# A two-layer graph network on one core: product 4 of the score projection split a second time by Strassen's scheme

## The chip, the cores and the metric

One core of a Trainium2 chip. The number that counts is the device time of one execution in microseconds (us); a single core runs, so it is that core's time. The engines are TensorE (PE in the profile, with its weight loads as PEld), VectorE (DVE), ScalarE (ACT), GpSimd (POOL) and SyncE (SP, which here only issues DMAs). Everything is fp32, apart from one product that uses fp32r.

## The reference

```python
# x: (64, 256, 512), adj: (256, 256) of zeros and ones, weights 512 x 512
h = max(layernorm(x), 0)
q, k, v = h @ Wq.T, h @ Wk.T, h @ Wv.T
rel = adj.T[None] * (q @ k.T)                 # per batch entry, 256 x 256
rel = rel / norm(rel, axis=2, keepdims=True)
x = x + rel @ v
h = max(layernorm(x), 0)
x = x + (einsum('nm,bmd->bnd', adj, h) @ weight + bias)
```

## The kernel before

The kernel takes the 64 batch entries two at a time: 32 pairs of 512 tokens. `M = Wq.T @ Wk` is made once, so the scores of a pair are `h M h.T`. For a pair there are: the transposed `h` (tile `ht`), G = the transpose of `h M` (tile `g`), V (tile `v`), the scores (`rel`), the attention product that is added to x, the second layer norm, y = adj times h2 (tile `yt`, "gather", in fp32r with h2 split into an upper and a lower part), and the product of y with the last weight, added to x ("mix").

Each large product is done by Strassen's scheme in Winograd's form: the two operands are cut in 2 x 2 blocks, sums of blocks are formed (the `left_factors` and `right_operands`, four sums each), and seven products of blocks take the place of eight. A product by one level here is 128x128 weights against 256 columns, four matmuls. The products of one result share a PSUM bank where one's value goes into the next: `bank_a` collects products 1, 6, 7 and 4, and after each of them VectorE or ScalarE takes the running sum out (`take`). For G, V and the mix, products 2 and 3 are split once more (`two_levels`, steps `g1` to `g4`): seven products of 128x128 against 128 columns, for 2 and 3 at once (`both`), in `bank_e` and `bank_d`, added into the first quarter of the result by VectorE (`add`). `bank_e` uses only its first half.

The second-level sums of the weights are made once by POOL (`second_right`). Those of h are made for each pair by VectorE (`second` in `new_ht`, called `h_second`, rows L176 to L179 with the tile `hs`). One level below, `sums` are the four first-level sums of h (rows L176 to L179 with the tile `ht`); the third gives factor 6, the fourth factor 3.

The transposes of h go by DMA and VectorE: `place_blocks` moves 32x32 blocks of h into the tile `blocks` (SP's queue), and `transpose_blocks` turns them, eight instructions a pair (L453). The last quarter of `blocks` is also scratch space of `norm_by_scalar` on ScalarE. `ident` is a 128x128 identity for transposes by matmul at the start and at the end.

The order of work on PE, DVE and ACT is the order of the code (`manual_schedule`); only waits on data are added. `run_steps` runs a list of PE steps, and after step n whatever stands in slot n of a dictionary. In `steady`, which makes 28 of the 32 pairs' rounds, one round is: `attend_and_v` (attention of pair i mixed with the rest of V of pair i+1), `scores` of pair i+1, `g_and_v` of pair i+2, the gather of pair i, and `mix_and_v`. What a slot holds is a matter of when VectorE and ScalarE get to it. In `g_and_v` the PE order is G's products 1, 5, 6 with g1, V's 1, G's 7 with g2, V's 5, G's 4 with g3; g4 of G comes in the mix. The bias is added to x by POOL (`add_bias`, L736), four adds a pair that wait only for their data: each may start when ScalarE's relu of the same chunk has read x (`relu_of`, L345). L566 is the mask (adjacency times scores), L580 the reciprocal of the norm, L583 the scaling of the scores, L720 and L724 the upper and lower part of h2. L469 and L490 are VectorE's takes and adds for G, L177 with the tile `yt` is the sum of y that product 5 of the mix needs.

Of the kernel before, what the change touches and what calls it, by code (L numbers as in the profile page):

```python
# [9 lines left out]
F32 = mybir.dt.float32  # L10
# [9 lines left out]
def kernel(  # L20
# [38 lines left out]
    nc = tc.nc  # L59
    P = 128  # L60
    B, N, D = x.shape
    DC = D // P
    NC = N // P
    NB = 2
# [5 lines left out]
    HC = DC // 2  # L70
# [8 lines left out]
    small = ctx.enter_context(tc.tile_pool(name="small", bufs=3))  # L79
    ps_m = ctx.enter_context(tc.tile_pool(name="ps_m", bufs=8, space=bass.MemoryType.PSUM))  # L80

    X, H, HL, G, V, R, H2, Y, HL2, Y2, second_h, own_steps = ({} for _ in range(12))

    ring = [const.tile([P, NB, NC, D], F32, name=f"x_ring{n}") for n in range(5)]
    blocks = const.tile([P, TC, DC, P], F32, name="blocks")
# [60 lines left out]
        t = const.tile([P, 3, HC, HD], F32, name=f"{name}_t")  # L146
        return right_operands(right_blocks(w), [t[:, n] for n in range(3)])

    def second_right(right, name):


        factors, steps = {}, []
        for n in (2, 3):
            t = const.tile([P, 3, P], F32, name=f"{name}_t{n}")
            factors[n], more = right_operands(
                lambda j, k, f=right[n]: f[:, j, ts(k, P)], [t[:, r] for r in range(3)], nc.gpsimd
            )
            steps += more
        return factors, steps

    def run(steps):
        for step in steps:
            step()
# [45 lines left out]

        return [(lambda args=args: step(*args)) for args in order]  # L210

    def two_levels(product, take, matmul, add):

        bank_a = ps_m.tile([P, 512], F32, tag="pm", name="bank_a")
        bank_c = ps_m.tile([P, 512], F32, tag="pm", name="bank_c")
        bank_d = ps_m.tile([P, 512], F32, tag="pm", name="bank_d")  # L220
        bank_e = ps_m.tile([P, 512], F32, tag="pm", name="bank_e")
        by_k = bank_d.rearrange("p (k s n) -> p k s n", k=2, s=2)
        at_b, at_c = by_k[:, :, 0], by_k[:, :, 1]
        at_a = bank_e[:, : 2 * P].rearrange("p (k n) -> p k n", k=2)

        def both(at, n, start=False):
            for k in range(2):
                matmul(at[:, k], k + 2, n, start and k == 0)

        def a1():  # L230
            product(bank_a, 1, True)
            take(0, 0, bank_a, True)

        def c5():
            product(bank_c, 5, True)
            take(1, 1, bank_c, True)

        def a6():
            product(bank_a, 6, False)
            take(0, 1, bank_a, True)  # L240

        def c():
            take(0, 1, bank_c, False)

        def a7():
            product(bank_a, 7, False)
            take(1, 1, bank_a, False)

        def a4():
            product(bank_a, 4, False)  # L250
            take(1, 0, bank_a, True)

        def g1():
            both(at_a, 1, True)
            both(at_c, 5, True)
            add(0, 0, at_a)
            add(1, 1, at_c)

        def g2():
            both(at_a, 6)  # L260
            both(at_c, 3)
            add(0, 1, at_a)

        def g3():
            both(at_a, 7)
            both(at_b, 2)
            add(1, 1, at_a)
            add(0, None, bank_d)

        def g4():  # L270
            both(at_a, 4)
            add(1, 0, at_a)

        return dict(a1=a1, c5=c5, a6=a6, c=c, a7=a7, a4=a4, g1=g1, g2=g2, g3=g3, g4=g4)

    def winograd(product, take, side={}, early=False):

# [126 lines left out]
    def new_ht(i):  # L404


        hh = twice.tile([P, DC * NC + 3 * HC, HT_], F32, tag="ht", name=f"ht_{i}")
        ht = hh[:, : DC * NC].rearrange("p (d h) n -> p d h n", h=NC)
        pair = hh[:, DC * NC : DC * NC + 2 * HC].rearrange("p (d e) n -> p d e n", e=2)
        HL[i], sums = left_factors(left_blocks(ht), [hh[:, DC * NC + 2 * HC :], pair[:, :, 1], pair[:, :, 0]])  # L410

        def second():
            room = work.tile([P, 4, 2, P], F32, tag="hs2", name=f"hs2_{i}")
            two = hh[:, HC * NC : DC * NC + 2 * HC].rearrange("p (w d e) n -> p w d e n", w=2, e=2)
            factors, steps = left_factors(
                lambda b, d: two[:, :, d, 0, ts(b, P)], [room[:, n] for n in range(4)]
            )
            HL2[i] = {k: {n: f[:, k - 2] for n, f in factors.items()} for k in (2, 3)}
            return steps

        second_h[i] = second
        return ht, sums

    def transposes_by_matmul(i):
# [51 lines left out]
    def g_by_two_levels(i):  # L476
        product, take = g_product(i)
        g = G[i].rearrange("p (k e) t n -> p k e t n", k=2)

        def matmul(out, k, n, start):  # L480
            nc.tensor.matmul(  # L481
                out, m_second[k][n], HL2[i][k][n], start=start, stop=True, skip_group_check=True
            )

        def add(b, e, sums):
            if e is None:
                dst, sums = G_all[:, :, 0, ts(b, P)], sums.rearrange("p (c n) -> p c n", c=DC)
            else:
                dst = g[:, :, e, 0, ts(b, P)]
            nc.vector.tensor_add(dst, sums, dst)  # L490

        G_all = G[i]
        return two_levels(product, take, matmul, add)

    def spare_blocks():

# [48 lines left out]
    def scores(i, side={}, by_matmul=False, inside=False, own=False):  # L545
# [61 lines left out]
        def turn_at_once():  # L607
            for b in range(NB):
                pt = ps_m.tile([P, T], F32, tag="pm", name="pr")
                for t in range(NC):  # L610
                    for k in range(NC):
                        nc.tensor.transpose(
                            pt[:, ts(t * NC + k, P)], rel[:, b, k, ts(t, P)], ident
                        )
                nc.scalar.copy(turned[:, b].rearrange("p t k n -> p (t k n)"), pt)

# [114 lines left out]
    def add_bias(i):  # L731

        xt = flat(X[i])
        add = nc.gpsimd.tensor_tensor
        return [
            (lambda c=c: add(xt[:, c, :], xt[:, c, :], bias_bc, ALU.add)) for c in range(TC)  # L736
        ]
# [169 lines left out]
    m_right, m_steps = weight_operands(m_sb, "m")  # L907
    wv_right, wv_steps = weight_operands(wvt_sb, "wv")
    w_right, w_steps = weight_operands(w_sb, "w")
    m_second, m_second_steps = second_right(m_right, "m2")  # L910
    wv_second, wv_second_steps = second_right(wv_right, "wv2")
    w_second, w_second_steps = second_right(w_right, "w2")
    in_order = {EngineType.PE, EngineType.DVE, EngineType.Activation}
# [14 lines left out]
    def g_and_v(i, side):  # L928

        g, v = g_by_two_levels(i), v_by_two_levels(i)  # L930
        run_steps([
            g["a1"], g["c5"], lambda: run([g["a6"], g["g1"]]), v["a1"],
            lambda: run([g["c"], g["a7"], g["g2"]]), v["c5"], lambda: run([g["a4"], g["g3"]]),
        ], side)
        return g, v

    def mix_and_v(i, g, v, side):


        m = mix_by_two_levels(i)  # L940
        run_steps([
            m["a1"], m["c5"], lambda: run([m["a6"], m["c"]]), lambda: run([m["g1"], v["a6"]]),
            lambda: run([m["a7"], m["g2"], g["g4"], v["c"]]), lambda: run([m["a4"], m["g3"]]),
        ], side)
        return m

    def first_pairs(exact):
# [42 lines left out]
            0: sums2[1:2], 1: sums2[2:3], 2: sums2[3:4],  # L990
        })
        stats, *parts = ln1(0, exact)
        h_second = second_h.pop(2)()
        attend(0, by_slot({c: [stats[c]] for c in range(TC)}, {
            0: masks[0:1], 1: masks[1:2] + squares[0:2], 2: squares[2:4] + [norm_root],
        }))
# [1 line left out]
        if exact:  # L998
            nc.vector.tensor_copy(adjt_r, adjt_sb)
        g, v = g_and_v(2, by_slot(layer_1(parts), {  # L1000
            1: h_second + [inverse], 2: turned3[0:4], 3: scales + [place],
            4: add_bias(0) + turned3[4:6], 5: turned3[6:8], 6: sums3[0:1],
        }))
        v_steps, rel_steps = attend_operands(1)
        y_products, y_steps = gather_steps(0, exact)
# [13 lines left out]
    def steady(i, exact, relu0, v_last, mixed, v):  # L1019
# [13 lines left out]
        if i + 4 < NP:  # L1033
            load(i + 4)
        HL2.pop(i + 1)
        h_second = second_h.pop(i + 2)()
        masks, squares, norm_root, inverse, scales, place, turns = scores(i + 1, {
            0: halves[2:3], 1: halves[3:4] + h_second[0:1], 2: [root] + h_second[1:4],
            3: [end] + relus[0:1], 4: relus[1:2],
        }, inside=True, own=True)  # L1040
        turned, sums = transpose_blocks(i + 3)
        v_steps, rel_steps = attend_operands(i + 1)
        g, v = g_and_v(i + 2, {
            0: masks + squares + [norm_root] + turned[0:4] + [inverse] + scales + [place],
            1: uppers[0:2] + lowers[0:2],
            2: relus[2:4],
            3: uppers[2:4] + turned[4:8],
            4: lowers[2:3] + sums[0:1] + add_bias(i),
            5: own_steps[i + 1][0:2] + lowers[3:4] + sums[1:3],
            6: own_steps[i + 1][2:4] + sums[3:4] + v_steps[0:1],  # L1050
        })
        y_products, y_steps = gather_steps(i, exact)
        run_steps(y_products, {0: v_steps[1:2], 2: y_steps[0:1], 3: turns})
# [14 lines left out]
    def last_pairs(exact, relu0, v_last, mixed, v):  # L1068
# [6 lines left out]
            0: v_last, 1: gs[0:1], 2: gs[1:2], 3: gs[2:3], 4: gs[3:4] + halves[0:1],  # L1075
            5: halves[1:2],
        })
        h_second = second_h.pop(c)()
        masks, squares, norm_root, inverse, scales, place, turns = scores(b, {
            0: halves[2:3], 1: halves[3:4] + h_second[0:1], 2: [root] + h_second[1:4],  # L1080
            3: [end] + relus[0:1], 4: relus[1:2],
        }, inside=True)
        g, v = g_and_v(c, {
            0: masks + squares + [norm_root, inverse] + scales + [place],
            1: uppers[0:2] + lowers[0:2],
            2: relus[2:4],
            3: uppers[2:4],
            4: lowers[2:3] + add_bias(a),
            5: lowers[3:4],
        })  # L1090
        y_steps = gather(a, exact)
        g["g4"]()
        gs = g_operands(c, spare_blocks())
        run_steps([v["a6"], v["g1"], v["a7"], v["g2"], v["a4"], v["g3"]], {
            0: gs[0:2] + [v["c"]], 1: gs[2:3], 2: gs[3:4], 3: y_steps[0:1], 4: y_steps[1:3],
# [83 lines left out]
```

## Time and profile before

| | |
|---|---|
| time, median of 3 runs | 1700.23 us (1699.68 to 1700.37) |
| profiled execution, its own time | 1700.89 us |
| its span, first to last instruction | 1699.1 us |
| TensorE clock granted, mean | 0.999 |
| one steady round (scores at 768.35 to scores at 820.08) | 51.73 us |
| in it busy: PE / DVE / ACT / POOL | 51.73 / 45.88 / 27.47 / 6.71 us |
| in its G stage (820.08 to 834.77): PE / DVE / ACT / POOL | 14.69 / 10.95 / 11.44 / 5.49 us |

The busy time of an engine is the union of its instructions' spans. Instructions of VectorE overlap a little, as do those of TensorE: a 128x512 sum lasts 0.68 us, and the next starts 0.60 us after it. So where cost is asked, the distance from start to start counts and not the duration. A wait in brackets at the end of a timeline line is the engine's idle time just before, with the instruction whose end is held to have released it. In the view of waits a line gives the total in us, how often, and the longest.

### The profile page before, as it was taken

The page shows a single profiled execution, that of the slowest core. Times are in us where ns is not written, and L with a number is a line of the kernel's source. Part 1 is how long each engine was busy: PE and PEld are TensorE (multiplying, and loading weights), DVE is VectorE, ACT ScalarE, POOL GpSimd, SP SyncE. Part 2 cuts the span into 40 slices and gives each one's busy share as a digit, 9 for nine tenths or more (in the row PEclk, how much of TensorE's full clock was granted, in tenths as well). Part 3 has the DMA queues.
Part 4 walks back from the last instruction along what each step waited for, and adds up shares of the span by engine and source line. Part 5 has one row for each costly group of instructions (what it writes and reads, how often), then busy time and mean ns, then how long its engine had stood idle before and what let it go on. Part 6 is the DMA issues. An engine that isn't in the chain of part 4 may idle for free.

```text
span 1699.1 us, 28457 instructions
## 1 busy us (share of the span) xinstructions
PE 1685.2 (99%) x10274; PEld 1530.6 (90%) x10274; DVE 1474.9 (87%) x3312; ACT 856.7 (50%) x1947; POOL 227.1 (13%) x191
## 2 busy tenths in 40 slices
PE   9999999999999999999999999999999999999998
PEld 7988999999999999999999999999999999999986
DVE  7788898888898888898888988888988889888777
ACT  4455445655545555446555456554465544564331
POOL 1211100111101111001111011110011110011111
PEclk9999999999999999999999999999999999999999
DMA  7413332233322233322333322333223333223101
GB/s 245 63 28 85 83 77 51 47 82 85 78 60 64 52 84 85 75 55 57 67 85 81 77 48 49 85 84 76 57 64 58 84 82 78 51 44 60 38 25 53
DMA packets 395270, 118.89 MB, mean 70 GB/s; under 512 B 367600, under 2 KB 368368, under 8 KB 395120
## 3 DMA queue, kind: packets, MB, share of 16 engines
q1 hardware_dynamic: 382528, 76.60, 24.1%
q0 software_dynamic: 8432, 32.51, 5.2%
q10 hardware_dynamic: 4160, 7.87, 1.3%
q8 instruction: 83, 1.36, 0.3%
q14 instruction: 67, 0.55, 0.1%
HBM read 38.27 MB, written 33.55 MB: 42 GB/s over the span
## 4 chain that ended last, share of the span: by engine, by line
PE 96%; DVE 3%; DMA 0%; issue 0%; ACT 0%; ACTq 0%; DVEq 0%
PE bank_a L302 25%; PE bank_a L290 13%; PE bank_a L314 7%; PE py L752 7%; PE bank_c L302 7%; PE bank_e L528 6%; PE bank_a L675 6%; PE bank_d L528 5%; PE bank_c L290 3%; PE bank_c L314 3%; PE bank_e L481 3%; PE bank_c L675 3%; PE bank_d L481 2%; PE bank_b L314 2%; PE bank_b L675 1%; PE pu L636 1%
## 5 line engine op out<-in xcount | busy, mean ns | idle before, releaser
L736 POOL TENSOR_TENSOR x_ring<-x_ring,bias_bc 128x512 f32<-128x512 f32 x128 | 187.6, 1486 | 667.6 <-DVE rel L563 436.3
L302 PE MATMUL bank_a<-wv_t,ht 128*128 128x256 f32 x768 | 181.7, 379 | 0.0
L290 PE MATMUL bank_a<-ht,m_t 128*128 128x256 f32 x768 | 181.4, 379 | 0.0
L290 PEld LDWEIGHTS bank_a<-ht,m_t 128*128 128x128 f32 x768 | 145.9, 190 | 19.8
L302 PEld LDWEIGHTS bank_a<-wv_t,ht 128*128 128x128 f32 x768 | 143.5, 190 | 18.3
L516 ACT COPY v<-bank_a 128x512 f32<-128x512 f32 x96 | 55.1, 574 | 206.5 <-PE bank_a L302 206.5
L724 DVE TENSOR_TENSOR h<-h2c,h 128x512 fp32r<-128x512 f32 x128 | 85.5, 691 | 80.1 <-ACT h L720 80.1
L367 ACT ACTIVATE blocks<-x_ring,sm 128x512 f32<-128x512 f32 x112 | 80.9, 722 | 119.4 <-DVE sm L364 117.6
L345 ACT ACTIVATE h2c<-x_ring,nb,rs 128x512 f32<-128x512 f32 x128 | 97.3, 808 | 59.7 <-DVE nb L342 50.0
L752 PE MATMUL py<-adjt_r,h 128*128 128x256 f32 x1024 | 126.0, 280 | 0.5 <-DVE h L724 0.4
L302 PE MATMUL bank_a<-w_t,ys 128*128 128x256 f32 x512 | 121.4, 380 | 0.4 <-DVE x_ring L786 0.3
L752 PEld LDWEIGHTS py<-adjt_r,h 128*128 128x128 f32 x1024 | 119.8, 188 | 1.0 <-DVE h L724 0.9
L807 POOL DMA_DIRECT2D out_dram<-x_ring x31 | 24.1, 776 | 720.5 <-issue 521.2
L380 ACT ACTIVATE h<-x_ring,nb,rs 128x512 f32<-128x512 f32 x112 | 82.0, 802 | 66.0 <-PE bank_e L528 66.0
L302 PEld LDWEIGHTS bank_a<-w_t,ys 128*128 128x128 f32 x512 | 96.8, 190 | 14.3 <-DVE x_ring L786 1.0
L786 DVE TENSOR_TENSOR x_ring<-bank_a,x_ring 128x512 f32<-128x512 f32 x128 | 88.0, 687 | 22.6 <-PE bank_a L302 22.5
L314 PE MATMUL bank_a<-ht,gt 128*128 128x128 f32 x744 | 101.2, 279 | 0.0
L561 ACT COPY rel<-bank_a 128x256 f32<-128x256 f32 x96 | 35.8, 373 | 129.7 <-PE bank_a L314 107.3
L333 DVE BATCH_NORM_STATS2 st<-x_ring 128x6 f32<-128x512 f32 x144 | 97.8, 679 | 0.4
L756 ACT COPY yt<-py 128x512 f32<-128x512 f32 x128 | 75.1, 588 | 45.4 <-PE py L752 44.5
L314 PEld LDWEIGHTS bank_a<-ht,gt 128*128 128x128 f32 x744 | 90.4, 192 | 3.0
L453 DVE STREAM_TRANSPOSE ht<-blocks 128x256 f32<-128x256 f32 x248 | 87.8, 409 | 0.8 <-DMA blocks<-h 0.8
(224 smaller groups left out, 4064.7 us busy)
## 6 DMA issues: line engine op xcount, KB each, us to landing
blocks<-h SPq DMA_DIRECT2D x496, 64.0 KB, 2.3
out_dram<-x_ring POOLq DMA_DIRECT2D x31, 1024.0 KB, 4.8
x_ring<-in_x_dram SPq DMA_DIRECT2D x28, 1024.0 KB, 5.7
placed<-rel SPq DMA_DIRECT2D x384, 32.0 KB, 2.0
x_ring<-in_x_dram ACTq DMA_DIRECT2D x4, 1024.0 KB, 5.4
wq_sb<-in_L_gnn_Wq_dram SPq DMA_DIRECT2D x4, 256.0 KB, 4.9
wk_sb<-in_L_gnn_Wk_dram ACTq DMA_DIRECT2D x4, 256.0 KB, 6.3
wv_sb<-in_L_gnn_Wv_dram ACTq DMA_DIRECT2D x1, 1024.0 KB, 5.8
```

The lines of the kernel that those rows point to most:

```text
L290: nc.tensor.matmul(bank[:, e * HT_ : (e + 1) * HT_], right[n][:, d, ts(e, P)], left[n][:, d, :], start=(start and e == 0 and d == 0), stop ...
L302: nc.tensor.matmul(bank[:, b * HD : (b + 1) * HD], left[n][:, d, ts(b, P)], right[n][:, d, :], start=(start and b == 0 and d == 0), stop=( ...
L314: nc.tensor.matmul(bank[:, ts(b, P)], right[n][:, d, ts(b, P)], left[n][:, d, ts(b, P)], start=(start and b == 0 and d == 0), stop=(d == H ...
L333: nc.vector.bn_stats(st[:, c, :], src[:, c, :])
L345: nc.scalar.activation(dst, src[:, c, :], AF.Relu, bias=nb[:, c : c + 1], scale=rs[:, c : c + 1])
L453: nc.vector.transpose(ht[:, d, half].rearrange("p (b n) -> p b n", b=NB), by_half[:, :, half, d])
L528: nc.tensor.matmul(out, left[k][n], right[k][n], start=start, stop=True, skip_group_check=True)
L675: nc.tensor.matmul(bank[:, ts(b, HD)], left[n][:, b], right[n][:, b], start=(start and b == 0), stop=True, skip_group_check=True,)
L724: nc.vector.tensor_sub(dst[:, 1, c, :], whole_h[c], dst[:, 0, c, :].bitcast(F32))
L736: (lambda c=c: add(xt[:, c, :], xt[:, c, :], bias_bc, ALU.add)) for c in range(TC)
L752: nc.tensor.matmul(pm[:, d, :], left[:, b * NC + m, ts(d0 + d, P)], right, start=(n == 0), stop=(n == len(terms) - 1),)
L786: nc.vector.tensor_add(xt[block], bank.rearrange("p (b e) -> p b e", b=NB), xt[block])
```

## The change

Product 4 of G is split a second time, like 2 and 3. Its seven quarter products are distributed so: numbers 2, 3 and 4 go straight into `bank_a` at the places of their quarters; numbers 1 and 5 go into the free second half of `bank_e`, and so do later 6 and 7, on top of 1. Steps `h1` (five matmuls, in the place of `a4`), `h1_sums` (two VectorE adds at the end of slot 6), `h2` (after product 5 of the mix) and `h3` (just ahead of `g4`).

For this, four sums of h at the second level are made for each pair (`fourth`, called `h_four`; they lie in the first quarter of `blocks`, once the transposes have read it), and four sums of the weight once more on POOL, one of which overwrites `ident`; so the last transposes by matmul take an identity made anew in `v_room`.

Other work moves. `h_second` goes from the scores to slot 0 of G, and the last two first-level sums of h from slots 5 and 6 of G to the scores of the next round (`late`). The transposes go from slots 0 and 3 to 1 and 3. Precision and data of the other products are as before.

```diff
-    def second_right(right, name):
+    def second_right(right, name, room=None):
         factors, steps = {}, []
-        for n in (2, 3):
-            t = const.tile([P, 3, P], F32, name=f"{name}_t{n}")
+        for n in (2, 3) if room is None else (2, 3, 4):
+            rooms = 3 if n < 4 else 2
+            t = const.tile([P, rooms, P], F32, name=f"{name}_t{n}")
+            t = [t[:, r] for r in range(rooms)] + [room]
...
+        four_a, four_c = bank_e[:, 2 * P : 3 * P], bank_e[:, 3 * P :]
+
+        def h1():
+            for n, at in ((2, 0), (3, 2), (4, 1)):
+                matmul(bank_a[:, ts(at, P)], 4, n, False)
+            matmul(four_a, 4, 1, False)
+            matmul(four_c, 4, 5, False)
+            take(1, 0, bank_a, True)
+
+        def h1_sums():
+            add_to_four(0, 0, four_a)
+            add_to_four(None, 1, four_c)
+
+        def h2():
+            matmul(four_a, 4, 6, False)
+            add_to_four(0, 1, four_a)
+
+        def h3():
+            matmul(four_a, 4, 7, False)
+            add_to_four(1, None, four_a)
...
+        def fourth():
+            room = blocks.rearrange("p c d e -> p (c d) e")
+            HL2[i][4], steps = left_factors(
+                lambda b, d: HL[i][4][:, d, ts(b, P)], [room[:, n] for n in range(4)]
+            )
+            return steps
...
+        def add_to_four(b, e, sums):
+            if b is None:
+                dst = G_all[:, e, 1, :].rearrange("p (b n) -> p b n", b=NB)
+            elif e is None:
+                dst = G_all[:, :HC, 1, ts(b, P)]
+            else:
+                dst = G_all[:, e, 1, ts(b, P)]
+            if b is None or e is None:
+                sums = sums.unsqueeze(1).to_broadcast([P, 2, P])
+            nc.vector.tensor_add(dst, sums, dst)
...
             g["a1"], g["c5"], lambda: run([g["a6"], g["g1"]]), v["a1"],
-            lambda: run([g["c"], g["a7"], g["g2"]]), v["c5"], lambda: run([g["a4"], g["g3"]]),
-        ], side)
+            lambda: run([g["c"], g["a7"], g["g2"]]), v["c5"], lambda: run([g["h1"], g["g3"]]),
+        ], by_slot(side, {6: [g["h1_sums"]]}))
...
-            m["a1"], m["c5"], lambda: run([m["a6"], m["c"]]), lambda: run([m["g1"], v["a6"]]),
-            lambda: run([m["a7"], m["g2"], g["g4"], v["c"]]), lambda: run([m["a4"], m["g3"]]),
+            m["a1"], lambda: run([m["c5"], g["h2"]]), lambda: run([m["a6"], m["c"]]),
+            lambda: run([m["g1"], v["a6"]]),
+            lambda: run([m["a7"], m["g2"], g["h3"], g["g4"], v["c"]]),
+            lambda: run([m["a4"], m["g3"]]),
...
@@ first_pairs @@
-            4: add_bias(0) + turned3[4:6], 5: turned3[6:8], 6: sums3[0:1],
+            4: add_bias(0) + turned3[4:6], 5: turned3[6:8] + h_four, 6: sums3[0:1],
...
@@ steady @@
-        h_second = second_h.pop(i + 2)()
+        make_second, make_four = second_h.pop(i + 2)
+        h_second = make_second()
+        sums = late.pop(i + 2, [])
         masks, squares, norm_root, inverse, scales, place, turns = scores(i + 1, {
-            0: halves[2:3], 1: halves[3:4] + h_second[0:1], 2: [root] + h_second[1:4],
+            0: halves[2:3], 1: halves[3:4] + sums[0:1], 2: [root] + sums[1:2],
             3: [end] + relus[0:1], 4: relus[1:2],
         }, inside=True, own=True)
+        h_four = make_four()
         turned, sums = transpose_blocks(i + 3)
+        late[i + 3] = sums[2:4]
         v_steps, rel_steps = attend_operands(i + 1)
         g, v = g_and_v(i + 2, {
-            0: masks + squares + [norm_root] + turned[0:4] + [inverse] + scales + [place],
-            1: uppers[0:2] + lowers[0:2],
+            0: masks + squares + [norm_root] + h_second + [inverse] + scales + [place],
+            1: uppers[0:2] + turned[0:6] + lowers[0:2],
             2: relus[2:4],
-            3: uppers[2:4] + turned[4:8],
+            3: uppers[2:4] + turned[6:8] + h_four,
             4: lowers[2:3] + sums[0:1] + add_bias(i),
-            5: own_steps[i + 1][0:2] + lowers[3:4] + sums[1:3],
-            6: own_steps[i + 1][2:4] + sums[3:4] + v_steps[0:1],
+            5: own_steps[i + 1][0:2] + lowers[3:4] + sums[1:2],
+            6: own_steps[i + 1][2:4] + v_steps[0:1],
         })
...
@@ last_pairs @@
         g, v = g_and_v(c, {
-            0: masks + squares + [norm_root, inverse] + scales + [place],
-            1: uppers[0:2] + lowers[0:2],
+            0: masks + squares + [norm_root] + h_second + [inverse] + scales + [place],
+            1: uppers[0:2] + h_four + lowers[0:2],
...
-        g["g4"]()
+        run([g["h2"], g["h3"], g["g4"], lambda: make_identity(nc, v_room[:, :P])])
```

## The prediction

> **What bounds the kernel now.** I read the busy times and the chain first, then the waits, then the timeline of one steady pair (its scores begin at 813.65 us, its G at 820.08).
>
> ```profile
> PE 1685.2 (99%) x10274; PEld 1530.6 (90%) x10274; DVE 1474.9 (87%) x3312; ACT 856.7 (50%) x1947; POOL 227.1 (13%) x191
> ...
> PE 96%; DVE 3%; DMA 0%; issue 0%; ACT 0%; ACTq 0%; DVEq 0%
> ```
>
> TensorE sets the end: it hardly ever stands still, and 96% of the chain is its matmuls. So only two things count: TensorE time taken out, and TensorE waits put in. VectorE has 13% idle on average, but the timeline of its instructions shows it packed from 783 to 819 us, with pauses of at most 0.4 us. Its one long rest (2.76 us) is in G.
>
> ```profile
> DVE h L724 <- ACT h L720: 80.1, 29, 2.8
> ...
> PEld bank_c L302 <- issue: 8.8, 29, 0.4
> ...
> PE bank_e L528 <- DVE x_ring L537: 3.3, 3, 1.6
> ```
>
> These are totals, times and longest of each wait; the first is VectorE's rest in G. The waits of PE itself in this view come to less than 10 us (the last line is the largest). But the second line is a warning: 29 times, once a pair, the weight load of product 5 of the mix comes late. The timeline shows for what: its operand is the sum L177, and VectorE ends that at 788.44, just as TensorE wants it.
>
> ```profile
> 787.79 0.65 DVE L177 TENSOR_TENSOR yt<-yt 128x512 f32<-128x512 f32 x1
> ...
> 788.59 1.10 PE L302 MATMUL bank_c<-w_sb,yt 128*128 128x256 f32 x4
> ```
>
> From end to first matmul are 0.15 us. Whatever makes VectorE later there makes TensorE later.
>
> **What the Trainium skill says.** "SBUF — State Buffer", section "Who interferes with whom": VectorE and GpSimd share a pair of SBUF ports; a VectorE instruction with two SBUF inputs and a GpSimd one that reads SBUF exclude each other, and the later one stands still until the earlier is over. The trace agrees. The bias adds on POOL (L736) alone take 1.27 us (the shortest of line L736); beside masks:
>
> ```profile
> 819.55 0.68 DVE L566 TENSOR_TENSOR rel<-rel,adjt_sb 128x512 f32<-128x512 f32 x1
> 819.63 3.42 POOL L736 TENSOR_TENSOR x_ring<-x_ring,bias_bc 128x512 f32<-128x512 f32 x2 [15.08 <-DVE rel L563]
> ...
> 820.69 1.23 DVE L566 TENSOR_TENSOR rel<-rel,adjt_sb 128x512 f32<-128x512 f32 x1 [0.45 <-ACT rel L561]
> ...
> 821.84 1.41 DVE L453 STREAM_TRANSPOSE ht<-blocks 128x256 f32<-128x256 f32 x4
> ```
>
> The same mask takes 0.68 alone and 1.23 where an add holds the ports; the two adds take 3.42 instead of 2.5. The transposes (one input) run at their usual pace. Near the end 128x128 sums meet two adds:
>
> ```profile
> 1668.11 2.68 POOL L736 TENSOR_TENSOR x_ring<-x_ring,bias_bc 128x512 f32<-128x512 f32 x2 [14.68 <-DVE ys L178]
> 1668.30 1.37 DVE L178 TENSOR_TENSOR ys<-ys 128x128 f32<-128x128 f32 x1
> ...
> 1669.71 1.24 DVE L179 TENSOR_TENSOR ys<-ys,ys 128x128 f32<-128x128 f32 x1
> ...
> 1671.33 0.38 PE L528 MATMUL bank_e<-w_t,ys 128*128 128x128 f32 x1 [1.42 <-DVE x_ring L537]
> ```
>
> They take turns: a sum of 0.28 us waits out one add, the next sum the next add, and TensorE then waits 1.42 us. "PSUM — Partial Sum Buffer", section "PSUM bank collisions raise a hardware error": two engines must not be on one bank at once, even in different columns, so such accesses have to be put in order. No row of before shows different columns.
>
> **The change, part by part.** *TensorE.*
>
> ```profile
> 823.54 1.89 PE L290 MATMUL bank_a<-ht,m_t 128*128 128x256 f32 x8
> 825.26 0.61 PE L481 MATMUL bank_e<-ht,m_sb 128*128 128x128 f32 x4
> 825.71 0.61 PE L481 MATMUL bank_d<-hs,m_sb 128*128 128x128 f32 x4
> ```
>
> (Each matmul of the code is two records.) From start to start, a product of four 256-column matmuls takes 1.72 us and two 128-column ones 0.445. Product 4 goes from four large (1.73) to seven small (7 x 0.2225 = 1.56): -0.17 a pair, -5 us in 30 pairs. Five are in h1 (1.11 for 1.73, -0.61 in G); h2 and h3 add 0.22 each in the mix.
>
> *VectorE, added.* Four 128x128 sums of h (h_four): the rows L176 to L179 at 128x128 have 281 to 321 ns and start 0.21 to 0.32 apart; 1.1 us for four that partly depend on each other. Four adds from PSUM: the two of 128x256 start 0.33 apart (L490); one of 128x128 from PSUM is not in the trace, at least 0.21 (the SBUF rows) and at most 0.33; I take 0.25. Sum 2.3 us a pair.
>
> *VectorE, moved.* Out of the scores: h_second (816.36 to 818.00, 1.64 us). Into them: two 128x512 sums, 0.6 each. Into slot 0 of G, ahead of the reciprocal L580: h_second, in the place of four transposes, which go to slot 1 where the 2.76 us rest was. Placing and landing of the blocks are done well before (last issue ends at 818.1), so transposes that come later wait for no DMA. SP's and ACT's queues get nothing new; POOL gets four small sums once, at the start, and an identity at the end.
>
> *What the moves meet.* L345's bias is ready 0.34 earlier, so its first relu ends at 819.2 and the first bias add starts at 819.3, ahead of mask 1. In turns: add to 820.55, mask 1 to 821.1, add to 822.2, mask 0 to 822.8, h_second (1.5) to 824.3. L580 starts there, not at 823.67: +0.6. (With the old order mask 0 ends at 821.9, the add holds h_second until 823.05, and it is 824.4.) Behind L580 wait ACT's four scales, the copy of bank_c and the casts L720, so the first L724 starts at 827.2 instead of 826.6; the six transposes (2.0) lie between for nothing. relu 2 ends at 828.9, bias adds 3 and 4 follow.
> VectorE: two L724 and two L490 to 829.1, two transposes to 829.75, then h_four. Add 3 holds the ports (829.0 to 830.25): the first sum passes at 830.4. Add 4 is next, to 831.55; the second sum ends at 831.7, the others at 832.25. Then come the takes of slot 4, before at 829.82: 2.43 late (0.6 from L580, 0.43 more work, 1.4 ports). The take of bank_a ends at 833.5, and h1 may write bank_a only then; TensorE wants it at 832.23. It had 1.15 us to spare (take over at 831.08), now it waits 1.3.
> From that take of bank_c to L177 were 9.71 us (829.82 to 839.53). Two sums of h with their gaps leave it (1.36), 0.35 of other gaps close, the first two adds from the shared bank and their gap come in (0.6): 8.6, so L177 starts at 840.85, 1.32 later than before. TensorE, without waiting, would be at product 5 of the mix 0.6 earlier than before; it is there 1.32 later.
>
> *In the mix.* h2 and h3: +0.45. g4 writes the low half of the bank whose high half VectorE reads for h3; put in order, it waits for that add. What such a turn costs:
>
> ```profile
> 1692.31 0.41 DVE L537 TENSOR_TENSOR x_ring<-bank_e,x_ring 128x256 f32<-128x256 f32 x1
> ...
> 1692.78 0.49 PE L528 MATMUL bank_e<-w_t,yt 128*128 128x128 f32 x2 [0.22 <-DVE x_ring L537]
> ```
>
> h3's second record starts 0.11 after the first and ends 0.275 later, the add starts 0.03 after that, takes 0.42, the matmul comes 0.05 after it and restarts 0.1 slower: 0.99, less the 0.22 of h3 itself, is 0.77. Behind g4 in TensorE's queue stands the whole rest of the mix. Bounds: 0 (not put in order) and 0.9 (VectorE not quite there). I take 0.77. The waits that VectorE has there (0.3 us before a take and before g4's add) hide the adds of h2 and h3.
>
> *Sum.* 1.32 + 0.45 + 0.77 = 2.54 us a pair, 28 pairs of the loop: 71.1. The first G has h_four one slot ahead of h1: it starts after the transposes (end 107.8) and TensorE, there at 105.6, waits about 3; +2.9 with the rest. In the last pair h2, h3 and g4 stand in a row, two turns: +1.5. Together +75.5 on 1700.89 (the profiled run; span 1699.1, 1.8 around it): **1776 us**. The profiled run is 0.7 above the median of 1700.23.
> Ends of the ports' cost a pair: 0 if adds and sums never meet, 3.1 if both adds of the second meeting are waited out in full (0.6 and two of 1.27); I take 0.6 and 1.4.
>
> **The rivals.**
> - *Ports, but no wait at g4*: for it, the columns differ and no row shows the wait; against it, the page. 75.5 less 28 x 0.77 and about 1.5 at the ends: 1753.
> - *Wait at g4, but no meeting on the ports*: the adds would have to fall beside transposes, as before. Against it: they follow relus 2 and 3 at once. Then L177 is 0.7 earlier, TensorE doesn't wait: -0.17 + 0.77 a pair, 17, with 4.4 at the ends: 1722.
> - *Faster*: VectorE's rests carry everything added; its takes in slot 4 come less than 1.15 us late, and g4 doesn't wait. Then TensorE keeps its -0.17 and loses the 0.1 late start at product 5: 28 x -0.27 + 2 for the first G, 1695. For it: the rest of 2.76 us in G is larger than 2.3. It turns at those 1.15 us.
> - *Worse*: later sums meet further waits, up to 1800.
>
> **How the numbers follow.** Forecast 0.56 (own range 1755 to 1788), ports alone 0.12, g4 alone 0.14, faster 0.13, worse 0.05. A difference under 0.2% (3.4 us) counts as none. Of the "faster" case 0.04 falls inside that, through the first G's wait. So faster 0.09, same 0.04, slower 0.87. The range, 1716 to 1788, leaves out the faster case, half of the worse one and some edges.
>
> **What would show it.** Of the four sums on `blocks`, about one takes 0.8 and one 1.3 us instead of 0.29, with an L736 beside each; TensorE waits for L469 in front of h1, some 1.3 us, 28 times; its wait in front of product 5 of the mix grows from 0.1 to over 1; a wait for the add of h3 of some 0.6 in front of g4; L580 0.6 later against the masks. It is wrong if TensorE's total of waits stays under 10 us, if h_four's sums take 0.3 each, or if L736 runs elsewhere.

## The result, and the profile after

The changed kernel takes 1777.62 us (median of 4, 1777.3 to 1779.04) against 1699.95 us for the kernel before: a ratio of 1.0454, 95% interval 1.0442 to 1.0467. Its profiled span is 1775.9 us. A steady round, from one pair's scores to the next, takes 54.24 us in place of 51.73: 28 times 2.5 us is 70 of the 78 us.

In the code after, line numbers have moved: the bias add L736 is now L783, the takes L469 and adds L490 of G are L504 and L525, the mask L566 is L613, the reciprocal L580 is L627, L724 is L771, the sums L176 to L179 are L178 to L181. The new adds from the shared bank are L538.

The page of the changed kernel, busy times and chain:

```profile
PE 1707.2 (96%) x10454; PEld 1531.1 (86%) x10454; DVE 1614.1 (91%) x3552; ACT 859.9 (48%) x1947; POOL 218.0 (12%) x197
...
PE 62%; DVE 25%; ACT 5%; issue 4%; SPq 1%; DMA 1%; DVEq 0%; ACTq 0%
```

TensorE was 96% of the chain before and is 62% now; VectorE has a quarter and ScalarE 5%. The busy time of VectorE grew by 139 us, far more than its new work: the last version below does that work in all pairs but one, and VectorE is busy for 1523.8 us. Nearly all of the other 90 us lies in instructions that stand still beside a bias add and count as busy: the masks last 1.56 us on average here and 0.85 there, the first two of the four new sums 0.94 and 0.28. TensorE's own waits (total us, times, longest), with the lines that were not there before:

```profile
PE bank_a L516 <- DVE g L504: 20.6, 28, 0.7
PE bank_e L516 <- DVE g L538: 15.9, 31, 0.5
PE bank_a L318 <- ACT g L502: 10.9, 29, 0.4
...
PE bank_a L516 <- DVE blocks L181: 3.0, 1, 3.0
PE bank_c L330 <- DVE yt L179: 2.8, 14, 0.5
```

In order: in front of h1, in front of g4, in front of product 7 of G, once in the first G, in front of product 5 of the mix. The first three come once a round. The totals understate the loss, since a matmul that had to wait also hands over to its successor late (below).

Where the waits come from is in the timeline of one round. It is the same pair as the example of before; at the start of G the two differ by 37.26 us (G begins at 857.34 here, at 820.08 there). The first meeting of POOL and VectorE (start, duration, instruction):

```profile
856.74 2.94 POOL L783 TENSOR_TENSOR x_ring<-x_ring,bias_bc 128x512 f32<-128x512 f32 x2 [14.75 <-ACT h2c L373]
856.99 3.24 DVE L613 TENSOR_TENSOR rel<-rel,adjt_sb 128x512 f32<-128x512 f32 x2
...
860.15 0.41 DVE L178 TENSOR_TENSOR hs<-ht 128x256 f32<-128x256 f32 x1
...
861.74 0.17 DVE L627 RECIPROCAL rn<-rn 128x4 f32<-128x4 f32 x1
```

The first add now starts ahead of mask 1. Two masks of 0.68 us each last 3.24 us together, and the reciprocal comes 4.40 us after the start of G. Before, it came 3.59 us after it:

```profile
823.67 0.18 DVE L580 RECIPROCAL rn<-rn 128x4 f32<-128x4 f32 x1 [0.42 <-ACT rn L577]
```

The second meeting, in the kernel after:

```profile
866.43 2.55 POOL L783 TENSOR_TENSOR x_ring<-x_ring,bias_bc 128x512 f32<-128x512 f32 x2 [6.75 <-ACT h2c L373]
...
867.23 0.62 DVE L178 TENSOR_TENSOR blocks<-ht 128x128 f32<-128x128 f32 x1
...
867.78 1.35 DVE L179 TENSOR_TENSOR blocks<-ht 128x128 f32<-128x128 f32 x1
...
869.17 0.29 DVE L180 TENSOR_TENSOR blocks<-blocks,ht 128x128 f32<-128x128 f32 x1
...
870.30 0.68 DVE L504 TENSOR_TENSOR g<-bank_a,g 128x512 f32<-128x512 f32 x1
...
871.04 0.49 PE L516 MATMUL bank_a<-ht,m_t 128*128 128x128 f32 x2 [0.73 <-DVE g L504]
```

Two of the four new sums take 0.62 and 1.35 us, the two after them 0.29, the price of such a sum alone. TensorE starts h1 0.06 us after the take of `bank_a` ends. In the mix, the turn at the shared bank:

```profile
888.02 0.39 PE L516 MATMUL bank_e<-blocks,m_t 128*128 128x128 f32 x2
...
888.45 0.42 DVE L538 TENSOR_TENSOR g<-bank_e,g 128x256 f32<-128x256 f32 x1
888.92 0.52 PEld L516 LDWEIGHTS bank_e<-ht,m_t 128*128 128x128 f32 x4 [0.71 <-DVE g L538]
888.92 0.71 PE L516 MATMUL bank_e<-ht,m_t 128*128 128x128 f32 x4 [0.52 <-DVE g L538]
...
889.47 1.25 PE L330 MATMUL bank_a<-w_t,yt 128*128 128x256 f32 x5
```

h3 starts at 888.02 and the product after g4 at 889.47: 1.45 us for what costs 3 x 0.2225 = 0.67 without a wait. The difference is 0.78. This is the price of the order; what would happen without it, no run here shows.

### The profile page after: what moved, and what is told of

Same layout as the page of the kernel before. It is cut to its first block, busy times and chain, and to the rows that moved or that the text cites. A ratio compares the mean times of both kernels' runs of the same rounds, so it can differ in the third digit from the quotient of the medians.

```text
span 1775.9 us, 29235 instructions
## 1 busy us (share of the span) xinstructions
PE 1707.2 (96%) x10454; PEld 1531.1 (86%) x10454; DVE 1614.1 (91%) x3552; ACT 859.9 (48%) x1947; POOL 218.0 (12%) x197
## 4 chain that ended last, share of the span: by engine, by line
PE 62%; DVE 25%; ACT 5%; issue 4%; SPq 1%; DMA 1%; DVEq 0%; ACTq 0%
PE bank_a L330 20%; PE bank_e L575 6%; PE bank_a L722 6%; PE bank_a L342 5%; PE bank_d L575 4%; PE bank_c L330 4%; PE py L799 4%; DVE h L771 3%; PE bank_e L516 3%; PE bank_c L342 3%; DVE rel L613 3%; ACT rel L630 3%; PE bank_c L722 3%; DVE g L525 2%; DVE blocks L179 2%
## 5 line engine op out<-in xcount | busy, mean ns | idle before, releaser
L783 POOL TENSOR_TENSOR x_ring<-x_ring,bias_bc 128x512 f32<-128x512 f32 x128 | 174.9, 1386 | 693.7 <-ACT h2c L373 679.0
L318 PE MATMUL bank_a<-ht,m_t 128*128 128x256 f32 x528 | 127.7, 385 | 10.9 <-ACT g L502 10.9
L318 PEld LDWEIGHTS bank_a<-ht,m_t 128*128 128x128 f32 x528 | 97.9, 190 | 34.7 <-ACT g L502 22.5
L771 DVE TENSOR_TENSOR h<-h2c,h 128x512 fp32r<-128x512 f32 x128 | 85.8, 693 | 20.9 <-ACT h L767 20.9
L613 DVE TENSOR_TENSOR rel<-rel,adjt_sb 128x512 f32<-128x512 f32 x64 | 97.7, 1562 | 0.0
```

The lines of the kernel that those rows point to most:

```text
L318: nc.tensor.matmul(bank[:, e * HT_ : (e + 1) * HT_], right[n][:, d, ts(e, P)], left[n][:, d, :], start=(start and e == 0 and d == 0), stop ...
L613: nc.vector.tensor_mul(rel[:, :, k], rel[:, :, k], adjt_sb[:, k : k + 1, :].to_broadcast([P, NB, N]))
L771: nc.vector.tensor_sub(dst[:, 1, c, :], whole_h[c], dst[:, 0, c, :].bitcast(F32))
```

## The experiments

The theory on record has two causes: meetings on the shared SBUF ports, and the turn at the shared PSUM bank in front of g4. Its main rival is that VectorE simply has too much to do. Round lengths are read from the traces, first score matmul to first score matmul.

**h3 early.** The step goes behind product 6 of the mix; nothing else changes.

```diff
-            m["a1"], lambda: run([m["c5"], g["h2"]]), lambda: run([m["a6"], m["c"]]),
+            m["a1"], lambda: run([m["c5"], g["h2"]]), lambda: run([m["a6"], g["h3"], m["c"]]),
...
-            lambda: run([m["a7"], m["g2"], g["h3"], g["g4"], v["c"]]),
+            lambda: run([m["a7"], m["g2"], g["g4"], v["c"]]),
```

> h3 and its add stand behind product 6 of the mix, so VectorE is done with the shared bank long before g4. If g4's wait for that add costs 0.77 us a round, 28 rounds give back 21.6: 1756 us, with the waits in front of h1 and of product 5 of the mix unchanged. If VectorE is late there anyway and the wait only shows it, the time stays within 5 us of 1777.

Measured: 1755.54 us (before on the same chip 1700.21; ratio 1.0324, interval 1.0306 to 1.0341). The rounds fall from 54.24 to 53.47, that is by 0.77 us. The waits in front of h1 and of product 7 stay; the one of g4 is left twice in all:

```profile
PE bank_a L516 <- DVE g L504: 20.8, 28, 0.7
PE bank_a L318 <- ACT g L502: 11.1, 29, 0.4
...
PE bank_e L516 <- DVE g L538: 0.9, 2, 0.5
```

The price of the turn is shown, and that it adds to the others.

**No bias adds**, with h3 late and with h3 early. The list of adds becomes a list of nothing:

```diff
-            (lambda c=c: add(xt[:, c, :], xt[:, c, :], bias_bc, ALU.add)) for c in range(TC)
+            (lambda: None) for c in range(TC)
```

> The changed kernel without the bias adds on POOL (the bias is left out of the output), so nothing holds the shared ports. If the ports make VectorE late (0.6 and 1.4 us a round), its takes come in time: no wait in front of h1 and almost none in front of product 5 of the mix, while g4 still waits: 1722 us (1715 to 1730). If VectorE's added work alone makes it late, the time stays above 1765.

> Both of the above: h3 early and no bias adds (the bias is left out of the output). If the two causes are separate and together all of the loss, only the shorter product 4 and the ends are left: 1697 to 1702 us. If there is a third cause in the rounds, over 1710.

Measured: 1715.30 us (1.0088, 1.0071 to 1.0104) and 1692.96 us (0.9957, 0.9941 to 0.9974), with rounds of 52.10 and 51.32. VectorE does all its added work in both, yet the waits in front of h1 and product 7 are gone, and the reciprocal is back at 3.59 us after the start of G, though `h_second` still stands ahead of it. The waits of TensorE with both causes taken away, the two longest:

```profile
PE bank_a L516 <- DVE blocks L181: 3.0, 1, 3.0
PE bank_e L575 <- DVE x_ring L584: 1.9, 2, 1.6
```

Neither belongs to a steady round. So the rival is out: it is not the amount of work on VectorE. The second time is 4 us below what was expected, a miss: rounds of 51.32 are 0.41 shorter than before, where the shorter product 4 gives 0.17 (see the last controls), and leaving the adds out is itself worth some 2.4 us after the last round, as the next run shows.

A control for the bias:

> Control: the kernel before without the bias adds (the bias is left out of the output). If the adds cost the kernel before nothing, 1699 to 1701 us, and the 7 us of the run with both causes taken away are the worth of the shorter product 4. If they cost it a part of the start of product 5 of the mix, 1695 to 1698, and that part is not product 4's.

Measured: 1698.22 us (0.9983, 0.9975 to 0.9990), between the two forecasts. Its rounds stay at 51.73; 2.4 us are gained after the last round, where two adds and 128x128 sums meet (the place shown in the prediction, where TensorE waited 1.42 us). In the rounds the adds cost the kernel before nothing, although a mask met one in each.

**The moves alone.** The kernel before, with product 4 by one level and only the new places of `h_second`, the first-level sums and the transposes.

```diff
-            0: masks + squares + [norm_root] + turned[0:4] + [inverse] + scales + [place],
-            1: uppers[0:2] + lowers[0:2],
+            0: masks + squares + [norm_root] + h_second + [inverse] + scales + [place],
+            1: uppers[0:2] + turned[0:6] + lowers[0:2],
...
```

> The kernel before with only the moves: second-level sums of h into slot 0 of G, two first-level sums into the scores, transposes into slots 1 and 3; product 4 by one level. If the first meeting on the ports (masks and second-level sums against the first two bias adds) costs by itself, ScalarE's copy of product 6 comes late and TensorE waits 0.4 to 0.5 us in front of product 7 of G in each of 28 rounds, partly won back at product 5 of the mix: 1707 to 1714 us. If the moves are harmless, 1696 to 1701.

Measured: 1712.93 us (1.0075, 1.0058 to 1.0092), rounds of 52.14. The only new wait of TensorE is this one:

```profile
PE bank_a L290 <- ACT g L467: 11.1, 29, 0.4
```

So the moves by themselves lose 0.41 us a round. The masks are late, and with them the reciprocal of the norm (4.40 us after the start of G, as in the changed kernel). ScalarE's queue waits for it, and the copy of product 6 that stands in this queue releases `bank_a` for product 7 too late.

**The four sums later.** In the changed kernel, `h_four` goes behind the takes of slot 4.

```diff
-            3: uppers[2:4] + turned[6:8] + h_four,
-            4: lowers[2:3] + sums[0:1] + add_bias(i),
+            3: uppers[2:4] + turned[6:8],
+            4: h_four + lowers[2:3] + sums[0:1] + add_bias(i),
```

> The changed kernel with one edit: the four new sums of h behind the takes of slot 4 instead of ahead of them. If the second meeting on the ports (1.4 us) is what makes the takes late and TensorE wait in front of h1, that wait goes, rounds fall from 54.24 to about 53.1 us and the time to 1740 to 1750; the waits in front of product 7 of G and of g4 stay. If VectorE's backlog from the first meeting is enough by itself, the wait in front of h1 stays and the time is above 1765.

Measured: 1739.19 us (1.0227, 1.0211 to 1.0243), rounds of 52.88: 1.36 us for one place in a list, a little more than expected (the time is 0.8 us below its range). TensorE's longest waits on VectorE and ScalarE for G:

```profile
PE bank_e L516 <- DVE g L538: 15.9, 31, 0.5
PE bank_a L318 <- ACT g L502: 11.0, 29, 0.4
```

The wait in front of h1 is gone, the two others are as they were. The edit takes two things from in front of the takes: the meeting, and the sums' own 1.05 us. It doesn't part them; the run without adds does, in which the sums stand in front of the takes and TensorE does not wait. No run has the second meeting without the first.

**Toward a version without the meetings, nothing left out.** First, h3 early, four transposes again in slot 0 beside the adds, `h_second` behind the reciprocal, `h_four` behind the takes; h1 takes its three products that need no new sum first.

```diff
-            0: masks + squares + [norm_root] + h_second + [inverse] + scales + [place],
-            1: uppers[0:2] + turned[0:6] + lowers[0:2],
+            0: masks + squares + [norm_root] + turned[0:4] + [inverse] + scales + [place],
+            1: uppers[0:2] + h_second + turned[4:6] + lowers[0:2],
...
```

> Nothing left out, bias adds as before; h3 early; four transposes again beside the first two bias adds, the second-level sums of h behind the reciprocal L580, and the four new sums behind the takes of slot 4, when the second two adds are nearly over. If loss is the meetings on the ports and the wait at g4 alone, a round takes 51.3 to 51.7 us and the kernel 1693 to 1703. If the new sums in themselves are too much for VectorE, rounds of over 52.5 and over 1715.

Measured: 1708.52 us (1.0042, 1.0028 to 1.0055), rounds of 51.81, a miss between the two forecasts. Mask 1 still meets the first add, because `h_second` is gone from the scores and the relu that releases that add comes earlier.

Then the ends:

```diff
-            lambda: run([g["c"], g["a7"], g["g2"]]), v["c5"], lambda: run([g["h1"], g["g3"]]),
...
+            lambda: run([g["c"], g["a7"], g["g2"]]), v["c5"], lambda: run([g["h1" if four else "a4"], g["g3"]]),
...
-        y_steps = gather(a, exact)
-        run([g["h2"], g["h3"], g["g4"], lambda: make_identity(nc, v_room[:, :P])])
+        y_products, y_steps = gather_steps(a, exact)
+        run_steps(y_products, {0: [g["h2"]], 2: [g["h3"]]})
+        run([g["g4"], lambda: make_identity(nc, v_room[:, :P])])
```

> The same, and the ends mended: the first pair's product 4 by one level (its four weight sums on POOL come after it), and the last pair's h2 and h3 between the products of its gather. The first round, 66.4 us in the changed kernel against 60.8 before, should fall to about 61 and the last by about 1: 4 to 6 us below the run without the mended ends, 1688 to 1698. If the long first round came from elsewhere, no difference.

Measured: 1703.43 us (1.0014, 1.0007 to 1.0020). The first round falls from 65.46 to 60.86 us, the last by 0.75, together the 5 us that were expected; the others stay at 51.81, so the time is above its range.

To bring the first add behind mask 1 again, one more sum was put into the scores:

```diff
-        late[i + 3] = sums[2:4]
+        late[i + 3] = sums[1:4]
...
```

> The run with the mended ends, with three instead of two first-level sums of h in the scores of the next round. The bias of the first relu is ready 0.6 us later, so the first bias add comes after mask 1 as in the kernel before, only mask 0 meets an add, and ScalarE's copy of product 6 is in time for product 7 of G. If the meeting of mask 1 is what is left of the loss, rounds fall from 51.81 to 51.3 to 51.5 us and the time to 1690 to 1698, below the kernel before. If the 51.81 come from VectorE's added work, no change or more: 1702 to 1710.

Measured: 1706.38 us (1.0038, 1.0024 to 1.0051), rounds of 51.9. A miss: the add does come behind mask 1 and the wait at product 7 is gone, but TensorE now waits in the scores, for the take that the third sum made late:

```profile
PE bank_a L343 <- DVE rel L611: 8.7, 29, 0.3
```

So the order of things, and not one sum more, had to do it. In the next run the bias for the relu is worked out after the take of product 7 of the scores, and a sum of v leaves the gather for the mix:

```diff
-            3: [end] + relus[0:1], 4: relus[1:2],
+            4: [end] + relus[0:2],
...
-        run_steps(y_products, {0: v_steps[1:2], 2: y_steps[0:1], 3: turns})
+        run_steps(y_products, {2: y_steps[0:1], 3: turns})
...
-            3: rel_steps[0:2] + row_squares[2:4], 4: root0 + rel_steps[2:4] + end0,
+            3: v_steps[1:2] + rel_steps[0:2] + row_squares[2:4], 4: root0 + rel_steps[2:4] + end0,
```

> The run with the mended ends and two moves more. The bias for the first relu is worked out behind the take of product 7 of the scores, not ahead of it, so the first bias add comes after mask 1 without any work added to the scores; and one sum of v goes from the gather into slot 3 of the mix, so L177's successor is ready 0.6 us earlier. If what was left in the rounds of 51.81 us is the meeting of mask 1 with an add and the start of product 5 of the mix, rounds take 51.2 to 51.5 us and the kernel 1688 to 1697, below the kernel before. If the freed 0.6 only comes back as a later take in the mix or the attention, rounds stay at 51.6 or more and the time at 1699 or more.

Measured: 1691.05 us against 1701.17 (0.9942, 0.9928 to 0.9955), rounds of 51.31 to 51.37. This version computes the whole reference and is faster than both kernels. VectorE at its two meetings, in the timeline of this run:

```profile
865.45 0.68 DVE L614 TENSOR_TENSOR rel<-rel,adjt_sb 128x512 f32<-128x512 f32 x1
866.76 1.05 DVE L614 TENSOR_TENSOR rel<-rel,adjt_sb 128x512 f32<-128x512 f32 x1 [0.63 <-ACT rel L609]
867.73 1.41 DVE L489 STREAM_TRANSPOSE ht<-blocks 128x256 f32<-128x256 f32 x4
...
876.47 0.28 DVE L178 TENSOR_TENSOR blocks<-ht 128x128 f32<-128x128 f32 x1
876.67 0.28 DVE L179 TENSOR_TENSOR blocks<-ht 128x128 f32<-128x128 f32 x1
```

One mask still meets an add (1.05 us instead of 0.68), which makes nobody late: the reciprocal comes 3.59 us after the start of G. The four sums take 0.28 to 0.29 us each.

How much of it is product 4? A control moves the sum of v in the kernel before:

> Control: the kernel before with one sum of v moved from the gather into slot 3 of the mix, product 4 by one level. If product 5 of the mix started 0.17 us late in each round because VectorE came late with its operand, rounds fall from 51.73 to about 51.56 and the time to 1695 to 1697; what the run with the new order gains beyond that belongs to product 4. If it gains as much as that run, 1690 to 1693, product 4 by two levels is worth nothing here; if 1699 to 1702, the late start had another cause.

Measured: 1698.95 us (0.9991, 0.9984 to 0.9997), rounds between 51.64 and 51.74. The fall, 1.55 us from 1700.5 and 0.05 us in the mean round, is about a third of what was expected. The gather and the first two products of the mix, taken together, last 7.36 us from start to start in the kernel before; here they last 7.28 or 7.33. The late start of product 5 goes, but in about half of the rounds the gather ahead of it takes 0.12 us longer, and in the others the matmuls after it still follow each other more slowly.

The distances between matmul starts, as means over the 28 rounds, account for the whole difference of 0.38 us between the kernel before and the new order. Product 4 by two levels gives 0.17. The gather and the first two products of the mix give 0.04. The scores give 0.18: a wait of TensorE in front of product 4 there and the slower matmuls after it, gone since `h_second` left the scores. The moves alone, with product 4 by one level, gain the same 0.18 there. The expectation would have put this down to product 4, as all that the control leaves over; so product 4 is worth its 0.17 us a round, and somewhat more than that came with the moves.

## Why the prediction held

The forecast of 1776 us was within 2 us of the time, and the sum per round (2.54) within 0.05 of the measured mean (2.49). To compare single moments, the scores are the right start, since VectorE's work in G follows from them; their starts lie 37.44 us apart in the two traces (813.65 and 851.09). By its steps:

- *Product 4 on TensorE.* The five matmuls of h1 and the two later ones run at 0.22 us each wherever TensorE doesn't wait. The 0.17 is real, but lost as long as VectorE sets the pace.
- *First meeting.* L580 was forecast at 824.3, and is at 861.74 less 37.44 = 824.30. What the prediction left out is that TensorE already feels this at product 7 of G: 0.64 us with its slow restart, by way of ScalarE's queue, shown by the moves alone. It changed no sum, because the same lateness would otherwise have been waited for at h1. There the wait is not 1.3 but about 0.9, and 1.2 with the slow restart.
- *Second meeting.* The sums were forecast to wait out the rest of one add and the whole of the next, and the takes to be 2.43 us late. Measured: 0.62, 1.35, 0.29, 0.29, and 869.70 less 37.44 = 832.26, which is 2.44 late.
- *L177.* Forecast at 840.85, measured 878.24 less 37.44 = 840.80. Product 5 of the mix comes 1.26 us later than before instead of 1.32.
- *g4.* 0.77 forecast, 0.78 in the trace, 0.77 when it was taken out.
- *A sign that did not come.* The wait in front of product 5 of the mix was to grow from 0.1 to over 1 us. In the mean round it is 0.28. The prediction's own sum gave less than its sign, about 0.7, and TensorE had already lost most of its time at product 7 and at h1, so it came to product 5 only a little before its operand was ready.
- *The first G.* The wait of 3 us is there, but the round is 5.6 us longer and not 2.9 (66.40 against 60.76). Three terms are missing from the sum: after the wait TensorE ran at half speed for 2.7 us (1.4 us lost, below), the turn at g4 comes in this round too (0.8), and VectorE's lateness met product 5 of the mix (0.5).
- *The faster rival.* It needed the takes in slot 4 in time and no turn at g4. Both were reachable by order alone, and then the kernel gains about as much as that rival said (1695 forecast, 1691 measured, with mended ends). That the sizes agree is partly chance: the rival knew nothing of the 0.18 us in the scores.
- *A gain it missed.* `h_second` out of the scores takes 0.18 us of waiting from TensorE there. The prediction saw no wait in the scores, and the view of waits of before has no line for one: the wait shows only in the distances between starts, of which the last two are 0.97 and 0.99 us before (G at 820.08) and 0.90 and 0.89 after (G at 857.34).

```profile
818.12 1.06 PE L314 MATMUL bank_b<-ht,g 128*128 128x128 f32 x8
819.09 1.16 PE L314 MATMUL bank_a<-ht,gt 128*128 128x128 f32 x8
...
855.55 1.06 PE L342 MATMUL bank_b<-ht,g 128*128 128x128 f32 x8
856.45 1.06 PE L342 MATMUL bank_a<-ht,gt 128*128 128x128 f32 x8
```

In the changed kernel this gain is not kept: TensorE is at G 0.18 us earlier, but the takes and L177 come when they were forecast, and it waits that much longer for them.

As means over the 28 rounds, the distances between matmul starts give the whole of it: 0.18 us less in the scores, 0.64 more at product 7 of G, 1.18 more at h1, 0.17 less for product 4, 0.23 more from the gather to product 5 of the mix, and 0.78 more at g4. That makes 2.48 of 2.49.

Inside a round, then, little of the agreement is luck. Over the whole run some is: the 2.7 us too little for the first G stand against 1.3 us too much for the 28 rounds (28 x 0.05) and 0.5 us by which the first scores start earlier in this execution than in the one of before.

## What to carry to other kernels

A list of work for VectorE is not only a matter of length: in these runs an instruction with two SBUF operands that fell beside a GpSimd add waited for the rest of it, while transposes and takes from PSUM beside the same adds ran at their usual pace (0.41 us a transpose, 0.65 to 0.69 a take). So put these there, and sums elsewhere. When a piece of work is taken out ahead of a GpSimd operation that starts on data, that operation moves too, and meets something else. Spare columns of a PSUM bank were free space here but not free order (0.78 us a turn): leave other work between one engine's read and the next engine's write of the same bank.

## What the runs showed of the hardware

After the wait in the first G, TensorE does not go on at its old rate. The timeline of the changed kernel:

```profile
105.05 0.38 PE L516 MATMUL bank_a<-ht,m_t 128*128 128x128 f32 x2
108.45 0.80 PE L516 MATMUL bank_a<-blocks,m_t 128*128 128x128 f32 x2 [3.01 <-DVE blocks L181]
109.03 0.63 PE L516 MATMUL bank_a<-ht,ident 128*128 128x128 f32 x2
109.46 0.64 PE L516 MATMUL bank_e<-ht,m_t 128*128 128x128 f32 x2
```

The small matmuls are 0.43 us apart instead of 0.22, until 111.17. The view of stretches gives the granted clock (the last number but two of a line):

```profile
105.05:108.45 3.40, 0.39 (x4) 0.19 (x2) 3.27 (x10) 1.53 (x4) 0.00 (x0) 0.92 0.15 19
108.45:111.61 3.16, 3.16 (x17) 3.16 (x17) 0.20 (x1) 0.59 (x1) 0.00 (x0) 0.55 0.35 52
111.61:115.34 3.73, 3.73 (x36) 3.73 (x35) 3.61 (x8) 1.76 (x3) 0.00 (x0) 1.00 0.34 48
```

A standstill of 3.0 us was followed by a clock of 0.55 over the next 3.2 us. The Trainium skill, "TensorE: Matmul & The Clock Gate", section "What's actually happening", describes such a gate, which halves the clock after an idle window of some 3.4 us; here a standstill somewhat shorter than that was enough. In the first run toward a version without the meetings the standstill was 2.6 us (to 109.60); the matmuls went on at their old pace for 1 us more, and then the clock was 0.64 from 111.60 to 115.00. The short waits of the rounds, up to 0.9 us, left the clock at 1.00. They cost something else: right after a wait the matmuls follow each other more slowly. Product 7 of G takes 1.83 us from start to start instead of 1.73, g4 0.55 instead of 0.445, and the first two matmuls of h1 together 0.72 instead of 0.445. So a wait costs more than the idle time that a view of waits reports.
